# Two-layer cross attention: the load of x issued after those of Wv and Wo, a split product in the first layer's queries, and key bias sums over all 800 query columns

## The chip, the cores and the metric

The kernel runs on one core of one Trainium2 chip. The metric is the device time of one execution in microseconds (us). Everything is float32.

## The reference

Two cross-attention layers run one after the other. There are 8 batches of 100 queries of width 1024 (x), and a context of 1444 rows of width 512 for each batch.

```
layer 0:  Q = x Wq + bq;  K = ctx Wk + bk;  V = ctx Wv + bv
          x = x + softmax_over_context(Q K^T / 32) V Wo + bo
layer 1:  q = x Wq + bq;  k = ctx Wk + bk;  v = ctx Wv + bv
          w = softmax_over_queries(q k^T / 32)
          out = layernorm(w v + x) * gamma + beta
```

## The kernel before

**What is multiplied.** Keys and values are never formed. Each layer first multiplies weights with weights: Wq Wk^T (1024 x 512, named `qk0` and `qk1`), and in layer 0 also Wv Wo (512 x 1024, `vo0`). `queries` then multiplies the transposed x (`xT`, 1024 x 800 in eight blocks of 128 rows) with the first product. The result `g0T` or `g1T` (512 x 800, kept as two halves of 400 columns) meets the raw context in `scores` (line 823). The softmaxed scores meet the raw context in `weighted_rows` (line 794), and `project0` or `project1` brings that back to width 1024.

**Split products.** The large products are done in seven half-size products in place of eight, with sums of blocks made on VectorE before and after. `inner_product` splits one of these seven once more in the same way: it makes eight block sums (named S1, T1 and so on in the code), runs seven products of a quarter of the size through `half_product`, and adds each to its place. It gives control back after each of the seven, so that a caller can weave other matmuls between them. In `queries` of layer 0 the product `A22 T1` (name `g0_w`) goes through `inner_product`, woven with eight single matmuls of `X += S3 T3`. The last one, `Y += S4 B22` (lines 702 and 703), is a plain product: 8 matmuls of 128x128 on 400 columns, and two VectorE additions into `g0T`.

**Loads.** A `unit` is one of 10 SBUF buffers 1536 columns wide. `weight_products` loads eight pairs of row blocks into eight units: for `vo0` the pair is Wv (256 KB) and Wo (512 KB), lines 354 and 355, on the queue of SyncE (SP). It yields once after writing down the loads. `qk0` holds eight units when `vo0` asks for its eight, so two of `vo0`'s pairs have a buffer at once and six wait for `qk0` to give one back. `xT` is a buffer of its own, loaded in two halves of 1600 KB at line 714, between the loads of `qk0` and those of `vo0`.

**Bias sums.** `transferred_sum` adds up a weight matrix scaled by a bias: eight ScalarE activations (line 524) into eight tiles, and seven accumulating DMAs from GpSimd's queue (line 528), each 512 KB, in a tree. This is done for `qk0` (`L0_xattn_bk`) and for `vo0` (`L0_xattn_bv`). `block_sums` transposes such a sum and reduces it on VectorE; for `vo0` that is written after the fifth step of the queries (line 743). `key_bias_sums` forms, for each query, the sum over 1024 features of `xT` times one scalar for each partition: per half of 400 columns one multiply (line 577) and seven multiply-adds (line 579), each of which reads what the one before wrote. Both layers call it once per half; its tile `kb` has three buffers. `key_biases` transposes the two halves and reduces them.

**What sets the order.** TensorE's instructions keep the order in which they are written (`manual_schedule(engines={PE})`). The order on the other engines and on their DMA queues is laid down by a planner when the program is built. `tc.keep_in_program_order`, and `vector.in_order = True` for the operations that go through `vector`, pin an instruction behind the one written before it on its engine. PSUM has six banks in the pool `psum` (`bank`) and two in `psum2` (`bank2`); a name that asks for a bank waits until one has been drained.

**Layer 1.** Its queries end with the plain product, too. Its `key_bias_sums` are written after five steps of the queries and are not pinned, so VectorE does them wherever the planner put them.

Of the kernel before, what the change touches and what calls it, by code (L numbers as in the profile page):

```python
# [31 lines left out]
P = 128  # L32
# [23 lines left out]
def two_layer_cross_attention(ctx: ExitStack, tc: tile.TileContext, a: dict, out: bass.AP):  # L56
# [83 lines left out]
    def run(*parts):  # L140

        parts = list(parts)
        while parts:
            parts = [g for g in parts if next(g, parts) is not parts]
# [387 lines left out]
    def block_sums(name, t, sums, late=False):  # L532

        ins = nc.vector.transpose(t, t)
        if late:
            tc.keep_in_program_order(ins)  # L540
        nc.vector.tensor_reduce(sums, t.rearrange("p (c q i) -> p c q i", q=P // QD, i=QD), AX.X, ALU.add)

    def totals(name, sums, n):

        ps = bank(name)[:, : n * P // QD]
        nc.tensor.matmul(ps, same, sums.rearrange("p c q -> p (c q)"), start=True, stop=True)  # L546
        own = small.tile([P, 2 * EC, P // QD], F32, tag="own", name=f"{name}_own", bufs=1)[:, :n, :]
        mask = quarter.unsqueeze(1).to_broadcast([P, n, P // QD])
        nc.vector.tensor_tensor(own, ps.rearrange("p (c q) -> p c q", q=P // QD), mask, ALU.mult)
        got = const.tile([P, n], F32, tag=name, name=name)  # L550
        nc.vector.tensor_reduce(got, own, AX.X, ALU.add)
        return got
# [14 lines left out]
        nc.vector.tensor_scalar(got, ps[:, :2], SCALE, None, ALU.mult)  # L567
        return got[:, 0:1], got[:, 1:2]

    def key_bias_sums(name, t0, t1, wqbk):  # L570

        acc = work.tile([P, GT + P - T], F32, tag="kb", name=name, bufs=3)
        nc.gpsimd.memset(acc[:, GT:], 0.0)
        for k in range(EC):
            src = xT[:, k, t0:t1]
            if k == 0:
                nc.vector.tensor_scalar(acc[:, :GT], src, wqbk[:, k : k + 1], None, ALU.mult)
            else:
                nc.vector.scalar_tensor_tensor(
                    acc[:, :GT], src, wqbk[:, k : k + 1], acc[:, :GT], ALU.mult, ALU.add  # L580
                )
        return acc

    def key_biases(name, kb, bqbk):

        sums = quarter_sums(name)[:, :B, :]
        t = row(f"{name}_t").rearrange("p (b q j) -> p b q j", q=P // QD, j=QD)
        for g in range(B // G):

            src = bass.AP(kb[g].tensor, kb[g].offset, [list(kb[g].ap[0]), [T, G], [QD, P // QD], [1, QD]])  # L590
            vector.transpose(t[:, g * G : (g + 1) * G], src)
        vector.tensor_reduce(sums, t, AX.X, ALU.add)
        yield
        c = totals(name, sums, B)
        nc.vector.tensor_scalar(c, c, SCALE, bqbk, ALU.mult, ALU.add)
        yield c

    def queries(layer, w, u):

        H, nb, h = EC // 2, 2, GT // 2
        A11, A12, A21, A22 = ([w[:, k * H : (k + 1) * H, j * 256 : j * 256 + 256]] for j in range(2) for k in range(2))
        B11, B21, B12, B22 = ([xT[:, k * H : (k + 1) * H, g * GT : g * GT + GT]] for g in range(2) for k in range(2))
        S1, S2 = ([row(f"g{layer}_s{n}").rearrange("p (c l) -> p c l", c=H)] for n in (1, 2))
        T1, T2 = ([wide(f"g{layer}_t{n}")] for n in (1, 2))
        T3 = [work.tile([P, LC, GT], F32, tag="gT", name=f"g{layer}_t3", bufs=3)]
        dst = [work.tile([P, LC, GT], F32, tag="gT", name=f"g{layer}T_{g}", bufs=3) for g in range(2)]

        def put(r, g, banks):
            for j in range(2):
                c = 2 * r + j
                nc.scalar.activation(dst[g][:, c, :], banks[j][:, :GT], AF.Identity, bias=u[:, c : c + 1])  # L614

        def add(r, g, banks):
            for j in range(2):
                to = dst[g][:, 2 * r + j, :]
                vector.tensor_tensor(to, to, banks[j][:, :GT], ALU.add)

        def parts(R, G):
            def part(r, c, ps):
                return dst[G][:, 2 * R + r, c * h : c * h + h], ps[:, :h]

            def put(r, c, ps):
                c0 = 2 * R + r
                nc.scalar.activation(*part(r, c, ps), AF.Identity, bias=u[:, c0 : c0 + 1])

            def add(r, c, ps):
                to, got = part(r, c, ps)  # L630
                vector.tensor_tensor(to, to, got, ALU.add)

            return put, add

        def pair(n):
            return [bank(f"g{layer}_{n}{j}") for j in range(2)]

        def product(banks, lhs, rhs, fresh):
            half_product(banks, lhs, rhs, fresh, nb, GT)

        t = unit(f"g{layer}_t")

        def inner(n, lhs, rhs, put, add, right=None):
            return inner_product(f"g{layer}_{n}", lhs, rhs, nb, GT, t, put, add, right)

        def steps():
            X = pair("x")
            product(X, A11, B11, True)
            put(0, 0, X)
            yield  # L650
            S3, S4 = A21, A12
            if layer == 0:
                Z = pair("z")
                product(Z, A12, B21, True)
            vector.in_order = layer == 0
            combine(S1, A21, A22, ALU.add)
            vector.in_order = True
            combine(T1, B12, B11, ALU.subtract)
            combine(S2, S1, A11, ALU.subtract)
            if layer == 0:  # L660
                combine(T2, B22, T1, ALU.subtract)
                vector.in_order = False
                yield
                vector.in_order = True
                add(0, 0, Z)
            combine(S3, A11, A21, ALU.subtract)
            if layer == 0:
                combine(T3, B22, B12, ALU.subtract)
            Y = pair("y")
            product(Y, S1, T1, True)  # L670
            put(1, 1, Y)
            if layer:

                vector.in_order = False
                yield
                vector.in_order = True
                S4 = A11
                combine(S4, A12, S2, ALU.subtract)
                _, more = parts(0, 0)
                room = [[T3[0][:, n, :].rearrange("p (i t) -> p i t", i=2)] for n in range(4)]  # L680
                Z = inner("z", A12, B21, more, more, room)
                combine(T2, B22, T1, ALU.subtract)
                run(Z)
                combine(T3, B22, B12, ALU.subtract)
            else:
                combine(S4, A12, S2, ALU.subtract)
            combine(T1, B21, T2, ALU.subtract)
            vector.in_order = False
            yield
            product(X, S2, T2, False)  # L690
            put(0, 1, X)
            yield
            vector.in_order = True
            V = half_steps(X, S3, T3, False, nb, GT)
            for _ in inner("w", A22, T1, *parts(1, 0)):
                next(V)
            run(V)
            add(1, 0, X)
            add(1, 1, X)
            vector.in_order = False  # L700
            yield
            product(Y, S4, B22, False)
            add(0, 1, Y)
            yield

        return dst, steps()
# [2 lines left out]
    *_, (wqk0, (acc_c, acc_u)) = weight_products(  # L709
        "qk0", "L0_xattn_WqT", "L0_xattn_WkT", E, L, (("L0_xattn_bk", 0), ("L0_xattn_bq", 1))  # L710
    )
    xT = const.tile([P, EC, B * T], F32, tag="xT", name="xT")
    for g in range(B // G):
        nc.sync.dma_start(
            out=xT[:, :, g * GT : (g + 1) * GT],
            in_=a["xT"].rearrange("(c p) t -> p c t", p=P)[:, :, g * GT : (g + 1) * GT],
        )
    bqbk0, bqbk1 = bias_products()
    sums_u, sums_c = quarter_sums("u0")[:, :LC, :], quarter_sums("c0")

    def first_block_sums():
        block_sums("u0", acc_u, sums_u, late=True)
        block_sums("wqbk0", acc_c, sums_c[:, :EC, :], late=True)

    *_, (wvo, (acc_o,)) = weight_products(
        "vo0", "L0_xattn_WvT", "L0_xattn_Wo", L, E, (("L0_xattn_bv", 1),), first_block_sums
    )
    gT = [None, None]
    gT[0], steps = queries(0, wqk0, totals("u0", sums_u, LC))
    got = []  # L730

    def key_biases_begun():
# [6 lines left out]
    run(islice(steps, 2))  # L739
    next(qk1)  # L740
    next(qk1)
    run(islice(steps, 3))
    block_sums("bvo", acc_o, sums_c[:, EC:, :], late=True)
    run(steps)
    wqbk0 = totals("wqbk0", sums_c, 2 * EC)
    nc.vector.tensor_tensor(out_bias, out_bias, wqbk0[:, EC:], ALU.add)
    kb0 = [key_bias_sums(f"kb0_{g}", g * GT, (g + 1) * GT, wqbk0[:, :EC]) for g in range(B // G)]
    wqk1, (acc_c, acc_u) = next(qk1)
    c0 = next(got[0])
    for t in prob:  # L750
# [376 lines left out]

    gT[1], steps = queries(1, wqk1, u1)
    run(islice(steps, 5))
    kb1 = [key_bias_sums(f"kb1_{g}", g * GT, (g + 1) * GT, wqbk1) for g in range(B // G)]  # L1130
    *_, key_bias[1] = key_biases("c1", kb1, bqbk1)
    vectors = [unit(f"vectors_{j}") for j in range(2)]
    gamma, beta = (t[:, :E] for t in vectors)
# [57 lines left out]
```

## Time and profile before

| what | value |
|---|---|
| median of 3 runs | 635.54 us (635.3 to 635.9) |
| profiled execution | 638.23 us |
| its span, first to last instruction | 636.1 us |
| mean granted TensorE clock | 0.995 |
| TensorE busy | 623.6 us, 98% |
| VectorE busy | 469.7 us, 74% |
| ScalarE, GpSimd busy | 165.9 us, 98.9 us |
| DMA | 138.32 MB, mean 217 GB/s |

All durations come from the one profiled execution, whose time is 638.23 us: its span of 636.1 us and 2.13 us around it. A matmul in float32 shows as two records[...]. Matmul records overlap, so the time of a group of them is taken from one start to the next.

### The profile page before, as it was taken

Reading aid. Unit: us, or ns where it says so; the run is one execution under the profiler, and the core shown is the slowest. Engines: PE = TensorE matmul, PEld = TensorE weight load, DVE = VectorE, ACT = ScalarE, POOL = GpSimd, SP = SyncE. Lnnn points to the kernel's source line nnn. Section 1 sums busy time; section 2 is a strip of 40 time slices with the busy share of each in tenths; the row PEclk is TensorE's granted clock in tenths of the full one; section 3 lists DMA queues with packets and bytes.
Section 4 is the critical chain, followed back from the end, with each engine's and each line's share of the span. In section 5 each row is a group of like instructions: output and inputs, shape, how many; then the busy total and the mean of one; then the engine's idle time right before and its main releaser. Section 6 shows DMA issues by size and latency. Waiting matters only on the chain.

```text
span 636.1 us, 10422 instructions
## 1 busy us (share of the span) xinstructions
PE 623.6 (98%) x4100; PEld 529.5 (83%) x4100; DVE 469.7 (74%) x942; ACT 165.9 (26%) x377; POOL 98.9 (16%) x131
## 2 busy tenths in 40 slices
PE   9999899999999999999999999999999999999994
PEld 8886366678985999999998656756999999999992
DVE  2956779977884797676655699639777659898886
ACT  1524210105204244323230001113432240325301
POOL 3112110002300000000000001007211220544054
PEclk9999999999999999999999999999999999999998
DMA  8999987015789888998965206156788990599002
GB/s 275 333 281 355 219 199 245 1 47 96 136 281 385 285 302 300 331 307 310 311 222 186 95 1 231 48 181 202 280 304 304 312 316 28 197 327 332 31 20 85
DMA packets 51943, 138.32 MB, mean 217 GB/s; under 512 B 4339, under 2 KB 8691, under 8 KB 51895
## 3 DMA queue, kind: packets, MB, share of 16 engines
q1 hardware_dynamic: 46792, 120.85, 55.1%
q0 software_dynamic: 4704, 16.35, 11.3%
q8 instruction: 32, 0.52, 0.3%
q10 hardware_dynamic: 398, 0.47, 0.2%
q14 instruction: 17, 0.13, 0.1%
HBM read 123.36 MB, written 3.28 MB: 199 GB/s over the span
## 4 chain that ended last, share of the span: by engine, by line
PE 93%; DMA 4%; DVE 1%; POOL 1%; issue 1%; POOLq 0%; ACT 0%; DVEq 0%; SPq 0%
PE s L823 25%; PE A L794 24%; PE qk_x L163 6%; PE g_x L163 5%; PE o_x L163 5%; DMA vo<-in_L_xattn_Wo 4%; PE g_y L163 3%; PE o_y L163 3%; PE qk_y L163 2%; PE qk_z L163 2%; PE vo_x L163 2%; PE o_w L163 2%; PE o_z L163 2%; PE qk_w L163 1%; PE vo_y L163 1%; PE z L1022 1%
## 5 line engine op out<-in xcount | busy, mean ns | idle before, releaser
L794 PE MATMUL A<-w,c 120*128 120x100 f32 (+1 forms) x1536 | 247.9, 266 | 0.0
L794 PEld LDWEIGHTS A<-w,c 120*128 120x128 f32 (+1 forms) x1536 | 216.2, 191 | 0.8
L96 DVE STREAM_TRANSPOSE w<-prob 32x384 f32<-32x384 f32 (+1 forms) x256 | 143.7, 561 | 35.1 <-ACT prob L835 15.7
L823 PE MATMUL s<-cT,g1T 128*100 128x131 f32 (+2 forms) x592 | 123.1, 297 | 0.3 <-DVE g1T L96 0.3
L823 PE MATMUL s<-cT,g0T 128*100 128x131 f32 (+2 forms) x592 | 122.9, 297 | 0.0
L823 PEld LDWEIGHTS s<-cT,g1T 128*100 128x100 f32 x592 | 78.4, 168 | 9.2 <-DVE g1T L96 1.2
L823 PEld LDWEIGHTS s<-cT,g0T 128*100 128x100 f32 x592 | 78.3, 168 | 8.4 <-PE c L546 0.4
L835 ACT ACTIVATE prob<-s,c 100x393 f32<-100x393 f32 (+2 forms) x64 | 35.0, 560 | 112.8 <-PE s L823 112.5
L945 ACT ACTIVATE w<-w,negmax 120x100 f32<-120x100 f32 (+1 forms) x96 | 34.8, 364 | 82.3 <-DVE negmax L96 82.3
L855 DVE TENSOR_REDUCE maxima<-prob 100x1 f32<-100x394 f32 (+3 forms) x32 | 16.5, 528 | 24.2 <-ACT prob L835 24.0
L1140 POOL DMA_DIRECT2D wv<-in_L_xattn_Wv x1 | 0.8, 772 | 203.2 <-PE o_x L163 203.2
L163 PE MATMUL qk_x<-qk 128*128 128x256 f32 x128 | 30.2, 384 | 0.0
L964 POOL TENSOR_TENSOR part<-w 120x500 f32<-120x500 f32 x8 | 10.9, 1366 | 113.0 <-DVE rstd L1039 28.6
L163 PEld LDWEIGHTS qk_x<-qk 128*128 128x128 f32 x128 | 23.8, 194 | 3.0 <-ACT qk L413 0.2
L528 POOL DMA_DIRECT2D qk_L_xattn_bk<-qk_L_xattn_bk x8 | 6.9, 863 | 102.5 <-ACT qk_L_xattn_bk L524 80.8
L614 ACT ACTIVATE g1T<-g_x,k 128x400 f32<-128x400 f32 x4 | 2.4, 594 | 69.1 <-PE g_x L163 68.9
L96 DVE TENSOR_TENSOR xT<-xT,o_x 128x400 f32<-128x400 f32 (+1 forms) x32 | 16.0, 541 | 4.1 <-PE o_x L163 3.9
L945 ACT ACTIVATION_READ_ACCUMULATOR w<-w,negmax 120x1 f32 (+1 forms) x96 | 17.9, 186 | 0.0
L1044 POOL TENSOR_TENSOR z<-z,vectors 100x1024 f32<-100x1024 f32 x7 | 16.5, 2358 | 8.2 <-ACT z L1043 8.2
L1043 ACT ACTIVATE z<-z,rstd 100x1024 f32<-100x1024 f32 x7 | 8.0, 1149 | 31.9 <-POOL rstd L1040 31.9
L1022 PE MATMUL z<-ident,xT 128*100 128x128 f32 x64 | 16.3, 273 | 0.0
L96 DVE TENSOR_TENSOR w<-w,rtotal 120x400 f32<-120x400 f32 (+1 forms) x24 | 15.6, 648 | 0.7
(319 smaller groups left out, 961.2 us busy)
## 6 DMA issues: line engine op xcount, KB each, us to landing
cT<-in_ctxT SPq DMA_DIRECT2D x64, 722.0 KB, 6.9
c<-in_ctx SPq DMA_DIRECT2D x48, 768.0 KB, 8.9
c<-in_ctx SPq DMA_DIRECT2D x16, 512.0 KB, 7.7
qk_L_xattn_bk<-qk_L_xattn_bk POOLq DMA_DIRECT2D x8, 512.0 KB, 8.3
vo<-in_L_xattn_Wo SPq DMA_DIRECT2D x8, 512.0 KB, 9.2
qk<-in_L_xattn_WqT SPq DMA_DIRECT2D x8, 512.0 KB
qk<-in_L_xattn_WqT SPq DMA_DIRECT2D x15, 256.0 KB, 6.0
c<-in_ctx SPq DMA_DIRECT2D x16, 224.0 KB, 5.3
```

The costliest lines, as they stand in the source:

```text
L96: ins = getattr(nc.vector, op)(*args, **kw)
L163: nc.tensor.matmul(banks[n // per][:, n % per * width : (n % per + 1) * width], lhs[i][:, n * P : (n + 1) * P], rhs[i], start=(fresh and i ...
L528: nc.gpsimd.dma_start(out=tiles[i], in_=tiles[i + n], accum_op=ALU.add)
L794: nc.tensor.matmul(ps[:, k * T : (k + 1) * T], c[m // CQ][:r, m % CQ, k * P : (k + 1) * P], w[:r, m, :], start=(m == 0 and k == 0), stop=( ...
L823: nc.tensor.matmul(banks[n // per][:T, cuts[n] - o : cuts[n + 1] - o], q[:, k, t0 : t0 + T], cT[k][:, cuts[n] : cuts[n + 1]], start=(k == ...
L835: nc.scalar.activation(p[:, part], ps[:T, : part.stop - part.start], AF.Identity, bias=key_bias[layer][:T, b : b + 1], scale=SCALE,)
L855: nc.vector.tensor_reduce(maxima[:, n : n + 1], p[:, part], AX.X, ALU.max)
L945: nc.scalar.activation(w[:r, m0 + m, :], w[:r, m0 + m, :], AF.Exp, bias=negmax[:r, m : m + 1], accum_out=total[:r, m : m + 1])
L964: add(part, w[:MR, 0:5, :], w[:MR, 5:10, :], ALU.add)
L1022: nc.tensor.transpose(ps[:T, e * P : (e + 1) * P], xT[:, 4 * j + e, b * T : (b + 1) * T], ident)
L1043: nc.scalar.activation(z, z, AF.Copy, scale=rstd)
L1044: nc.gpsimd.tensor_tensor(z, z, beta[:T], ALU.add)
```

## The change

Three things are done.

1. The loads of `vo0` are written first, by the first step of `weight_products`, and the two halves of `xT` after them. The rest of `vo0` follows as before.
2. In layer 0 the last product of the queries, `S4 B22`, goes through `inner_product` under the name `q`, with the tile `T2` as room for its right-hand block sums. For that, `add(0, 1, Y)` moves ahead of it, into the loop over the steps of `w`; the first product of `q` is woven in before the last matmul of `X += S3 T3`, and the additions of `X` come behind the fifth of the seven. `block_sums("bvo", ...)` moves from its place behind the fifth step into that loop, as `between`. Layer 1 keeps the plain product.
3. `key_bias_sums` runs over all 800 columns at once: one multiply and seven multiply-adds in place of two and fourteen, in one buffer in place of three; `key_biases` transposes once.

```diff
-    def key_bias_sums(name, t0, t1, wqbk):
-        acc = work.tile([P, GT + P - T], F32, tag="kb", name=name, bufs=3)
+    def key_bias_sums(name, wqbk):
+        acc = work.tile([P, B * T + P - T], F32, tag="kb", name=name, bufs=1)
         for k in range(EC):
-            src = xT[:, k, t0:t1]
...
-                    acc[:, :GT], src, wqbk[:, k : k + 1], acc[:, :GT], ALU.mult, ALU.add
+                    acc[:, : B * T], xT[:, k, :], wqbk[:, k : k + 1], acc[:, : B * T], ALU.mult, ALU.add
...
-            for _ in inner("w", A22, T1, *parts(1, 0)):
+            for n, _ in enumerate(inner("w", A22, T1, *parts(1, 0))):
                 next(V)
...
+                if layer == 0 and n == 1:
+                    between()
+                elif layer == 0 and n == 3:
+                    add(0, 1, Y)
+                    _, more = parts(0, 1)
+                    Q = inner("q", S4, B22, more, more, four(T2[0]), 768)
+            if layer == 0:
+                next(Q)
+                run(V)
+                yield
+                run(islice(Q, 4))
+                add(1, 0, X)
+                add(1, 1, X)
+                run(Q)
+                vector.in_order = False
+            else:
...
+vo0 = weight_products(
+    "vo0", "L0_xattn_WvT", "L0_xattn_Wo", L, E, (("L0_xattn_bv", 1),), first_block_sums
+)
+next(vo0)
 xT = const.tile([P, EC, B * T], F32, tag="xT", name="xT")
 for g in range(B // G):
     nc.sync.dma_start(
...
+*_, (wvo, (acc_o,)) = vo0
...
-run(islice(steps, 3))
-block_sums("bvo", acc_o, sums_c[:, EC:, :], late=True)
 run(steps)
...
-kb0 = [key_bias_sums(f"kb0_{g}", g * GT, (g + 1) * GT, wqbk0[:, :EC]) for g in range(B // G)]
+kb0 = key_bias_sums("kb0", wqbk0[:, :EC])
...
-kb1 = [key_bias_sums(f"kb1_{g}", g * GT, (g + 1) * GT, wqbk1) for g in range(B // G)]
+kb1 = key_bias_sums("kb1", wqbk1)
```

More of the change, by code (lines that the diff above doesn't have):

```diff
@@ L568, in bias_products @@
         return got[:, 0:1], got[:, 1:2]
-    def key_bias_sums(name, t0, t1, wqbk):
-        acc = work.tile([P, GT + P - T], F32, tag="kb", name=name, bufs=3)
-        nc.gpsimd.memset(acc[:, GT:], 0.0)
+    def key_bias_sums(name, wqbk):
+        acc = work.tile([P, B * T + P - T], F32, tag="kb", name=name, bufs=1)
+        nc.gpsimd.memset(acc[:, B * T :], 0.0)
         for k in range(EC):
-            src = xT[:, k, t0:t1]
             if k == 0:
-                nc.vector.tensor_scalar(acc[:, :GT], src, wqbk[:, k : k + 1], None, ALU.mult)
+                nc.vector.tensor_scalar(acc[:, : B * T], xT[:, k, :], wqbk[:, k : k + 1], None, ALU.mult)
             else:
                 nc.vector.scalar_tensor_tensor(
-                    acc[:, :GT], src, wqbk[:, k : k + 1], acc[:, :GT], ALU.mult, ALU.add
+                    acc[:, : B * T], xT[:, k, :], wqbk[:, k : k + 1], acc[:, : B * T], ALU.mult, ALU.add
                 )
@@ L587, in key_biases @@
         t = row(f"{name}_t").rearrange("p (b q j) -> p b q j", q=P // QD, j=QD)
-        for g in range(B // G):
-            src = bass.AP(kb[g].tensor, kb[g].offset, [list(kb[g].ap[0]), [T, G], [QD, P // QD], [1, QD]])
-            vector.transpose(t[:, g * G : (g + 1) * G], src)
+        src = bass.AP(kb.tensor, kb.offset, [list(kb.ap[0]), [T, B], [QD, P // QD], [1, QD]])
+        vector.transpose(t, src)
         vector.tensor_reduce(sums, t, AX.X, ALU.add)
@@ L596, in key_biases, with queries @@
         yield c
-    def queries(layer, w, u):
+    def queries(layer, w, u, between=None):
         H, nb, h = EC // 2, 2, GT // 2
@@ L641, in queries, with inner, four @@
         t = unit(f"g{layer}_t")
-        def inner(n, lhs, rhs, put, add, right=None):
-            return inner_product(f"g{layer}_{n}", lhs, rhs, nb, GT, t, put, add, right)
+        def inner(n, lhs, rhs, put, add, right=None, at=0):
+            return inner_product(f"g{layer}_{n}", lhs, rhs, nb, GT, t[:, at:], put, add, right)
+        def four(t):
+            return [[t[:, n, :].rearrange("p (i t) -> p i t", i=2)] for n in range(4)]
         def steps():
@@ L679, in steps @@
                 _, more = parts(0, 0)
-                room = [[T3[0][:, n, :].rearrange("p (i t) -> p i t", i=2)] for n in range(4)]
-                Z = inner("z", A12, B21, more, more, room)
+                Z = inner("z", A12, B21, more, more, four(T3[0]))
                 combine(T2, B22, T1, ALU.subtract)
@@ L694, in steps @@
             V = half_steps(X, S3, T3, False, nb, GT)
-            for _ in inner("w", A22, T1, *parts(1, 0)):
+            for n, _ in enumerate(inner("w", A22, T1, *parts(1, 0))):
                 next(V)
[L697 to L703, printed above, removed]
+                if layer == 0 and n == 1:
[14 more added lines that the diff above has]
+            else:
+                run(V)
+                add(1, 0, X)
+                add(1, 1, X)
+                vector.in_order = False
+                yield
+                product(Y, S4, B22, False)
+                add(0, 1, Y)
             yield
@@ L711, in two_layer_cross_attention, with first_block_sums @@
     )
+    bqbk0, bqbk1 = bias_products()
+    sums_u, sums_c = quarter_sums("u0")[:, :LC, :], quarter_sums("c0")
+    def first_block_sums():
+        block_sums("u0", acc_u, sums_u, late=True)
+        block_sums("wqbk0", acc_c, sums_c[:, :EC, :], late=True)
+    vo0 = weight_products(
+        "vo0", "L0_xattn_WvT", "L0_xattn_Wo", L, E, (("L0_xattn_bv", 1),), first_block_sums
+    )
+    next(vo0)
     xT = const.tile([P, EC, B * T], F32, tag="xT", name="xT")
@@ L717, in two_layer_cross_attention @@
         )
[L718 to L726, printed above, removed]
-    )
-    gT = [None, None]
-    gT[0], steps = queries(0, wqk0, totals("u0", sums_u, LC))
+    *_, (wvo, (acc_o,)) = vo0
+    gT = [None, None]
+    gT[0], steps = queries(
+        0, wqk0, totals("u0", sums_u, LC), lambda: block_sums("bvo", acc_o, sums_c[:, EC:, :], late=True)
+    )
     got = []
```

## The prediction

> **What bounds the kernel now.** I read the page's busy times first, then who TensorE waited for, then the chain that ended last.
>
> ```profile
> PE 623.6 (98%) x4100; PEld 529.5 (83%) x4100; DVE 469.7 (74%) x942; ACT 165.9 (26%) x377; POOL 98.9 (16%) x131
> ...
> PE vo_z L163 <- DMA vo<-in_L_xattn_Wo: 2.8, 1, 2.8
> PE warm L108 <- DVE ones L105: 1.1, 1, 1.1
> PE s L823 <- DVE g1T L96: 0.3, 1, 0.3
> ```
>
> The second part (engine, what it waited for: total, times, longest) is complete: TensorE stands still 4.2 us in all. So only two things gain time: less work on TensorE, or the 2.8 us of waiting for Wo in `vo0`. Everything else is cover. The chain, in order of time (start, us, what), shows both places:
>
> ```profile
> 43.72 9.32 DMA vo<-in_L_xattn_Wo
> 53.08 14.77 DMA vo<-in_L_xattn_Wo
> 67.98 1.96 PE vo_z L163 x4
> ...
> 132.45 0.68 PE g_w_x L163 x4
> 133.12 1.34 PE g_x L163 x4
> 134.47 5.37 PE g_y L163 x16
> ```
>
> The last Wo block, issued at 53.08, lands at 67.85, and `vo_z` wanted it at 65.2. `g_y` at 134.47 is the product that the change splits. Third, SP's queue in order of time: x goes out at 17.81, two pairs of Wv and Wo behind it, and then SP stands for 13 us until `qk0` gives buffers back.
>
> ```profile
> 17.81 1.08 SPq L714 DMA_DIRECT2D xT<-in_xT  x2
> 19.03 5.19 SPq L354 DMA_DIRECT2D vo<-in_L_xattn_WvT  x1
> 24.27 1.10 SPq L355 DMA_DIRECT2D vo<-in_L_xattn_Wo  x1
> 25.42 0.48 SPq L354 DMA_DIRECT2D vo<-in_L_xattn_WvT  x1
> 25.95 2.57 SPq L355 DMA_DIRECT2D vo<-in_L_xattn_Wo  x1
> 41.62 0.33 SPq L354 DMA_DIRECT2D vo<-in_L_xattn_WvT  x1
> ```
>
> In stretches of 2 us the DMA share is 0.9 to 1.1 from 2 to 72 us, without a gap. What sets the landing of the last Wo is thus the bytes ahead of it, not its issue.
>
> [...] the seventh Wo landed at 61.42, 1.9 us after the sixth, when SP's queue was nearly alone; the eighth took 6.4 us more, with two accumulating DMAs of GpSimd's queue (issued from 57.35) under way. [...] three linked multiply-adds of 400 columns in layer 1 take (1.94-0.63)/2 = 0.655 us each, two chains in turn in layer 0 (7.73-0.63)/13 = 0.546 us.
>
> **Part 1, the order of the loads.** No DMA is added; two (3.28 MB) move. Written order would put them behind all eight pairs. But the planner does not keep written order where an instruction is ready early. In GpSimd's order of time:
>
> ```profile
> 5.46 0.20 POOL L138 MEMSET prob<- 128x4 f32 x3
> 5.56 0.26 POOL L573 MEMSET kb<- 128x28 f32 x3
> 23.88 0.92 POOL L528 DMA_DIRECT2D qk_L_xattn_bk<-qk_L_xattn_bk  x1 [18.07 <-ACT qk_L_xattn_bk L524]
> ```
>
> Line 573 is written far behind the accumulating DMAs of line 528 (one of the three belongs to layer 1), needs no input, and ran at 5.56 us because its buffer was free; the fourth, for which none was, ran at 178.4. The load of x needs no input either, its buffer is free from the start, and it isn't pinned. When SP has issued the second pair, the third has no buffer until about 41 us. So I take it that x goes out there, at about 21 us, behind two pairs of eight. Nothing on SP waits behind it in that gap.
>
> Then the same bytes lie ahead of the last Wo: 6.29 MB of `qk0`, x, and the pairs. DMA stays busy without a gap, the buffers come back when TensorE gives them (41.62 to 52.7), and the wait stays. The first two pairs land some 10 us earlier than 45.7 and 48.9, and TensorE wants them at 53 and later. Value: 0. The bounds are -2.76 (x behind all eight) and +2.25 (a third accumulating DMA of `vo0` gets in ahead, priced below).
>
> **Part 2, the split product.** TensorE: 8 matmuls of 400 columns, 16 records in 5.37 us, go. Seven products of 2 matmuls on 200 columns come, 4 records each, 0.68 us each by the rows of `g_w` (0.672 between starts): 4.7 us. Gain 0.65 us on the path. In layer 1 the same seven stand alone in `g_z` at 0.68, so weight loads don't slow them.
>
> VectorE gets eight block sums (four of 256 columns at 0.34, four of 400 at 0.48, from start to start in `g_w`): 3.3 us; and eight additions of 200 columns at 0.28: 2.2 us. The two additions of Y stay and only move. The cover:
>
> ```profile
> 131.88 0.36 DVE L96 TENSOR_TENSOR g0T<-g0T,g_w_y 128x200 f32<-128x200 f32 x1 [3.01 <-PE g_w_y L163]
> ```
>
> 3.0 us idle here and 0.9 before the next. I lay the pinned order on the clock of before. The block sums of `w` end at 127.6. The transpose and reduction of `bvo` (1.17 and 1.14) end at 129.9, the additions of Y (moved) at 131.0, the first four sums of `q` at 132.6. The additions of `w` follow as TensorE delivers, to 133.7. The first product of `q` ends at 134.5; its addition and two sums end at 135.6, wanted by the fourth product at 136.5. The next pair ends at 137.0; TensorE wants its first half, done at 136.6, at 137.2. Slack 0.5 to 0.9 us: no wait. The four additions of X run from 138.2 to 140.1 and give back the banks of X. `qk1`'s first product would start at 139.4 and needs its second bank at 140.2; the first of X is free at 139.6. Slack 0.6 us. If the planner puts a filler of `qk1` (0.34 to 0.61 us) in the wrong place, TensorE waits some tenths: 0 to +1.0, taken +0.1.
>
> **Part 3, the key bias sums.** VectorE only. In layer 0 they took 141.64 to 150.04, 8.4 us. One chain of 800 exposes the link at each step: [...] 8.0 us. So the gain is 0.4 us on VectorE, not half. They end at about 149.8, since part 2 ends 0.5 us later on VectorE. TensorE next wants VectorE's sums for `qk_y` at 153.2, chunk by chunk; up to 3 us of these remain: near, but covered.
>
> In layer 1 a step over 800 columns needs both halves of `xT`, and blocks 4 and 5 of the second half are finished at about 384 and 385.
>
> ```profile
> 386.22 1.94 DVE L579 SCALAR_TENSOR_TENSOR kb<-xT,k,kb 128x400 f32<-128x400 f32 x3
> 388.27 0.71 DVE L96 STREAM_TRANSPOSE c_t<-kb 128x512 f32<-128x512 f32 x1
> 389.01 1.22 DVE L96 TENSOR_REDUCE c_sums<-c_t 128x32 f32<-128x1024 f32 x1
> 390.15 1.22 DVE L96 TENSOR_TENSOR qk<-qk,g_s 128x1024 f32<-128x1024 f32 x1
> ...
> 395.70 0.36 DVE L96 TENSOR_TENSOR g1T<-g1T,g_z_x 128x200 f32<-128x200 f32 x1 [0.96 <-PE g_z_x L163]
> ```
>
> Before, five steps of 400 came after 384.02; now four of 800 must (about 4.2 us with their links, against 3.1), and one transpose of 1.17 for two (1.33). So the sum at 390.15, which the split `g_z` needs, starts up to 0.9 us later. The 0.96 us idle at 395.70 takes that: 0, with bounds -0.1 and +1.0. Without that cover it is one for one, for TensorE already waits 0.3 us in `g_z` on this chain.
>
> **Sum.** 0 - 0.65 + 0.1 = -0.55 us. The profiled execution would go from 638.23 (span 636.1) to 637.7; the median, 2.7 us lower than the profiled time, from 635.54 to 635.0.
>
> **The rivals.** A: x really goes out behind all eight pairs. Then the DMA engines have 3.28 MB less ahead of Wo. By 28 us they had moved 8.7 MB; without x they run out at about 35.5 us, 6 us before the next buffer. From 41.62 on, 4.72 MB of pairs and up to 2.1 MB of accumulations at the 325 GB/s of 42 to 68 us take 21 us: the last Wo lands at about 63 at the latest, and `vo_z` wants it at 65.2. The wait goes, x lands before 80 and is wanted at 102.6. 635.0 - 2.8 = 632.2. For it: the written order. Against it: the memsets.
>
> B, slower: the first two pairs land early, ScalarE scales them early, and a third accumulating DMA of `vo0` is issued before the last Wo lands. Its price is (6.4-1.9)/2 = 2.25 us, estimated from the two that were under way. 635.0 + 2.25 = 637.25; it decides from 1.9 us of extra wait on. For it: GpSimd's queue was held by the tree of `qk0` until 56.81, after the first tiles of `vo0` were ready. Against it: the third step needs the first two landed, or tile 5, scaled only at 60.6.
>
> C: a bank or a late block sum in part 2, or the chain of 800 in layer 1, costs TensorE more than the split gains: 1.0 to 1.7 us of new waits, 636.2 (up to 636.9). For it: slacks of 0.5 to 1 us at four places. Against it: each of these holds on paper.
>
> **How the numbers follow.** Forecast 0.58, A 0.19, B 0.14, C 0.09. A measurement of this kernel tells 0.2%, 1.27 us, from no change. The forecast's own range is 634.2 to 636.2; 0.52 of it is no change and 0.06 faster (a wait for Wo that shrinks). A is faster. B is slower. C is 0.04 no change and 0.05 slower. Faster 0.25, same 0.56, slower 0.19. The range of 8 in 10, 632.2 to 637.2, cuts A and B in half and leaves out a few in a hundred beyond.
>
> **What would show it.** SP's order of time: x between the second and third pair (part 1), or behind the eighth at about 54 us (A). TensorE's wait for Wo: 2.8 as before, none (A), about 5 (B). `g_q` in seven pieces of 0.68 us and no new wait of `g_q` or `qk_x` on VectorE or on a bank. The multiply-adds of 800 columns at about 1.07 us from start to start. `g_z` in layer 1 without more than 0.3 us of waits. The prediction is wrong if x is where it is written, or if VectorE's order around 128 to 141 us is another than the one laid out.

## The result, and the profile after

| | median | runs | all runs |
|---|---|---|---|
| before | 636.01 us | 20 | 635.01 to 641.68 |
| changed | 641.42 us | 20 | 634.05 to 644.48 |

The ratio of changed to before is 1.0055, with a 95% interval of 1.0031 to 1.0079: slower, by half a per cent. It compares mean times, 640.79 with 637.27 us, and leaves out the two longest runs of the changed kernel, which count as slow; the medians differ by 5.4 us. The prediction was 635.0 us, with a range of 632.2 to 637.2. Both kernels scatter by several us, and the scatter belongs to the case: 6 of the 20 runs of before lie above 638 us, and 19 of the 20 of the changed kernel.

The profiled execution of the changed kernel took 640.21 us, its span is 638.4 us and its mean granted clock 0.992. First, whom TensorE waited for (engine, what it waited for: total us, times, longest):

```profile
PE vo_z L163 <- DMA vo<-in_L_xattn_Wo: 4.5, 1, 4.5
PE warm L108 <- DVE ones L105: 1.1, 1, 1.1
PE s L843 <- DVE g1T L96: 0.3, 1, 0.3
```

There is no new entry. The old one, the wait for the last Wo, grew from 2.8 to 4.5 us. The chain in order of time (start, us, what) passes the same two loads as before:

```profile
43.09 12.17 DMA vo<-in_L_xattn_Wo
55.27 13.65 DMA vo<-in_L_xattn_Wo
```

The fourth Wo, out at 43.09, takes 12.17 us where it took 9.32. The last one goes out when the fourth has landed, as before, so at 55.27 where it was 53.08. Behind it comes the surprise: the four records of the last pair of `vo_z` take 3.63 us, against 1.96 before. TensorE's own order of time has the wait in brackets, and the windows of 1 us (length, TensorE's busy time and records, granted clock, DMA share, GB/s) have the reason:

```profile
69.06 3.63 PE L163 MATMUL vo_z<-vo 128*128 128x512 f32 x4 [4.47 <-DMA vo<-in_L_xattn_Wo]
```

```profile
67.00:68.00 1.00, 0.00 (x0) 1.00 1.10 268
...
69.00:70.00 1.00, 0.94 (x1) 0.51 1.07 258
...
72.00:73.00 1.00, 1.00 (x3) 0.79 0.44 170
```

After standing for 4.47 us TensorE ran at half its clock (0.50 to 0.51) for 3.4 us. Before, after 2.76 us, the clock stayed at 1.00. In this execution the longer wait cost 1.67 us once more, after it was over.

SP's queue in order of time shows that x went where the prediction put it, between the second pair and the third:

```profile
19.83 0.33 SPq L355 DMA_DIRECT2D vo<-in_L_xattn_Wo  x1
20.85 2.47 SPq L743 DMA_DIRECT2D xT<-in_xT  x2
40.99 0.34 SPq L354 DMA_DIRECT2D vo<-in_L_xattn_WvT  x1
```

The split product is as laid out, in pieces of 0.67 us (0.84 us of record, overlapping), with some 0.15 us more around `g_q_w` (139.08, 139.82 and 140.57 are the starts from the piece ahead of it on). In layer 1 VectorE's order of time answers to the rows shown of before:

```profile
387.94 3.23 DVE L578 SCALAR_TENSOR_TENSOR kb<-xT,k,kb 128x800 f32<-128x800 f32 x3
391.27 1.25 DVE L96 STREAM_TRANSPOSE c_t<-kb 128x1024 f32<-128x1024 f32 x1
392.44 1.18 DVE L96 TENSOR_TENSOR qk<-qk,g_s 128x1024 f32<-128x1024 f32 x1
...
398.05 0.36 DVE L96 TENSOR_TENSOR g1T<-g1T,g_z_x 128x200 f32<-128x200 f32 x1
```

Three linked steps of 800 columns take 3.23 us, (3.23 - 1.04)/2 = 1.09 us from start to start, and the idle 0.96 us ahead of the addition of `g_z_x` is used up. With the span longer by 2.3 us, the sum at 392.44 stands where it stood (390.15).

The bill of the two profiled executions: wait +1.71, half clock +1.67, split product -0.50 (from the start of `vo_y` to that of `qk_x` 69.57 us, where it was 70.07; weighed below), and TensorE was done with the pair ahead of the last one 0.63 us earlier (65.22 to 64.59), the cause of which is open. That makes +2.25 of the +2.3 us in the span.

### The profile page after: what moved, and what is told of

The parts are those of the page before. It is cut to its first block, busy times and chain, and to the rows that moved or that the text cites. A ratio compares the mean times of both kernels' runs of the same rounds, so it can differ in the third digit from the quotient of the medians.

```text
span 638.4 us, 10446 instructions
## 1 busy us (share of the span) xinstructions
PE 624.2 (98%) x4112; PEld 530.7 (83%) x4112; DVE 472.5 (74%) x940; ACT 165.8 (26%) x377; POOL 98.8 (15%) x129
## 4 chain that ended last, share of the span: by engine, by line
PE 90%; DMA 4%; DVE 3%; issue 1%; POOL 1%; POOLq 0%; ACT 0%; DVEq 0%; SPq 0%
PE s L843 25%; PE A L814 24%; PE qk_x L163 6%; PE o_x L163 5%; PE g_x L163 4%; DMA vo<-in_L_xattn_Wo 4%; PE o_y L163 3%; PE qk_z L163 2%; PE qk_y L163 2%; PE vo_x L163 2%; PE g_y L163 2%; PE o_z L163 2%; PE o_w L163 2%; PE qk_w L163 1%; PE vo_y L163 1%; PE z L1042 1%
```

## Where the loss comes from: part 1 or the rest

**e1_order_only** is the kernel before with part 1 alone. **e2_rest_only** is the changed kernel with x loaded where it was, that is, parts 2 and 3 alone.

```diff
 e1_order_only, against the kernel before
-    xT = const.tile(...)
-    for g in range(B // G): nc.sync.dma_start(...)
...
+    next(vo0)
+    xT = const.tile(...)
+    for g in range(B // G): nc.sync.dma_start(...)
+    *_, (wvo, (acc_o,)) = vo0
```

```diff
 e2_rest_only, against the changed kernel
+    xT = const.tile(...)
+    for g in range(B // G): nc.sync.dma_start(...)
     bqbk0, bqbk1 = bias_products()
...
     next(vo0)
-    xT = const.tile(...)
-    for g in range(B // G): nc.sync.dma_start(...)
```

> The kernel before with the changed order of loads alone (x behind the second pair of Wv and Wo, as the planner puts it); queries and key bias sums as before. Theory W (the new place of x makes the last Wo land later; TensorE stands longer than 4 us, and then runs at half clock for some 3 us): 5 us slower than before, about 641 us, wait of vo_z for Wo 4 us or more, and records of vo_z at double length. Theory V (the loss is in the split product or in VectorE's sums, and the longer wait is chance, since the kernel before also has executions of 640 us): within 1 us of before, with the same mixture of times.

> The changed kernel with x loaded where it was, ahead of Wv and Wo: split product and wide key bias sums alone. Theory W: 0.65 us faster than before, about 635.3 us, wait for Wo 2.8 us as before. Theory V: slower than before, up to 5 us, with new waits of TensorE in g_q, qk_x or qk_y.

e1_order_only: 642.77 us (640.8 to 644.38), ratio 1.0084 [1.0064, 1.0104], wait for Wo 4.8 us, and after it a granted clock of 0.58 and 0.56 in the windows from 70 to 72 and from 72 to 74 us. e2_rest_only: 636.7 us (634.06 to 641.49), ratio 1.0003 [0.9977, 1.0029], and no wait for Wo at all in its profiled execution (634.96 us), where theory W had 2.8; 8 of its 20 runs lie above 638 us. So the loss is part 1's. Parts 2 and 3 can't be weighed against a scatter of 7 us.

## Is it the place of x in the queue, and what does the half clock cost?

**e3_x_behind_all** is the changed kernel with the two loads of x pinned, so that they stand behind all eight pairs (rival A of the prediction). **e4_kept_busy** has five matmuls that nobody reads ahead of the last pair of `vo_z`; they only fill the wait.

```diff
 e3_x_behind_all, against the changed kernel
-        nc.sync.dma_start(out=xT[...], in_=...)
+        tc.keep_in_program_order(nc.sync.dma_start(out=xT[...], in_=...))
```

```diff
 e4_kept_busy, against the changed kernel
-            product(Z, A12, B21, True)
+            zs = half_steps(Z, A12, B21, True, nb, rh)
+            run(islice(zs, 3 * nb))
+            fill = bank("fill")
+            for _ in range(5):
+                nc.tensor.matmul(fill, units[4][:, :P], units[4][:, l_width : l_width + 512], ...)
+            run(zs)
```

> The changed kernel with the two loads of x pinned in written order behind all eight pairs. Theory W: no wait for Wo in vo_z (last Wo lands at about 63 us), no stretch at half clock: 632.2 us and little spread from execution to execution. Rival: the last Wo still lands after 65 us, since the two accumulating DMAs issued at 57 us set it and not the bytes of x: 635 us or more, with a wait of 1 us or more. Theory V: 3 us or more above 632.2 although no wait for Wo is left.

> The changed kernel with five extra matmuls of 128x128 on 512 columns (4.3 us, into a bank that nothing reads) ahead of vo_z's last pair, so that TensorE isn't idle while it waits for the last Wo. It tells the half clock from the wait. If standing still is what lowers the clock: no records at half clock, the remaining wait under 1 us, and 1.7 to 3 us faster than the changed kernel, about 638.5 to 639.5 us. If the clock has nothing to do with standing still: the stretch at half clock stays, and the time is that of the changed kernel (641.4) or above.

e3_x_behind_all: 636.81 us (636.05 to 639.08), ratio 0.9984 [0.9963, 1.0004]. That is 4.6 us less than the changed kernel, but 4.6 us more than the 632.2 that rival A was given. TensorE still waits, now at the sixth pair:

```profile
63.89 5.76 PE L163 MATMUL vo_z<-vo 128*128 128x512 f32 x12 [1.99 <-DMA vo<-in_L_xattn_Wo]
```

The accumulating DMAs of `vo0` started at 47.21 and 53.92 in this kernel, since its first pairs landed early, and from 54 to 62 us, in windows of 2 us, the DMA engines moved only 246 to 290 GB/s. The 325 GB/s that rival A took from the kernel before didn't hold, and the last Wo landed at 67.7 us, not by 63.

e4_kept_busy: 640.16 us (638.15 to 645.83), ratio 1.0049 [1.0024, 1.0074]. The median is 1.3 us under the changed kernel's 641.42, but the two were not measured side by side, and by the ratios (1.0049 against 1.0055) a gain in time is not shown. TensorE's order of time, the filling matmuls and the last pair behind them:

```profile
66.21 4.46 PE L468 MATMUL fill<-vo 128*128 128x512 f32 x10
71.50 1.96 PE L163 MATMUL vo_z<-vo 128*128 128x512 f32 x4 [0.83 <-DMA vo<-in_L_xattn_Wo]
```

The last Wo came later still (71.4), yet the last pair took 1.96 us at a clock of 1.00. So in this case it is standing still that lowers the clock, and as an estimate (1.67 us of the 5.4 between the medians) that is the smaller part of the loss. What the filling saves is less in some runs: five of the 20 took 642.8 to 645.8 us, at a mean clock of 0.991 to 0.994, where the other 15 have 0.995 to 0.998. What makes Wo late was still only argued: the accumulating DMAs beside it.

## The accumulating DMAs of vo0 held back

In these four kernels the accumulations of `vo0` go out from the last tiles to the first, pinned. The first of them then waits until the last Wo has landed and been scaled, and none of them is under way while Wv and Wo are loaded. Work and bytes are the same. The edit is put on the kernel before (e5), on e2_rest_only (e6), on the changed kernel (e7) and on e3_x_behind_all (e8).

```diff
 e5 to e8, in transferred_sum
-            for i in range(0, EC, 2 * n):
-                nc.gpsimd.dma_start(out=tiles[i], in_=tiles[i + n], accum_op=ALU.add)
+            order = range(0, EC, 2 * n)
+            for i in reversed(order) if name.startswith("vo0") else order:
+                ins = nc.gpsimd.dma_start(out=tiles[i], in_=tiles[i + n], accum_op=ALU.add)
+                if name.startswith("vo0"):
+                    tc.keep_in_program_order(ins)
```

> The kernel before, with one thing added: the accumulating DMAs of vo0 go out from the last tiles to the first and are pinned in that order, so that none of them is under way while SP still loads Wv and Wo. Same work, same bytes. Theory W (what delays the last Wo is that SP's queue shares the DMA engines with the first accumulations of vo0): the last Wo, issued at about 53, lands some 2 us after the seventh, by 64 us; no wait of vo_z above 0.3 us, no half clock, span about 633.3 and 635 or less, and nearly the same time in every run (within 1.5 us). Rival R (the last Wo is late because of where its issue stands in SP's queue, or because of the bytes ahead of it): the wait for Wo stays at 1 us or more in the profile, and the time at 636 to 637 with its spread.

> Parts 2 and 3 alone (x at its old place), with the accumulations of vo0 held back as in e5_hold_before. With the wait for Wo out of the way this weighs parts 2 and 3. My prediction had -0.65 us on TensorE and +0.1 us of new waits, and the traces showed 0.35 us less outside the span: e5_hold_before minus 0.5 to 1.0 us, about 634. A rival: they cost as much as they gain, and this is within 0.2 us of e5_hold_before.

> The changed kernel with the accumulations of vo0 held back. Theory W: x behind the second pair costs only by way of the race of the last Wo with the accumulations of vo0; without the race the last Wo, issued at about 55, lands by 65 us, the wait is under 0.5 us, and the time is that of e6_hold_rest within 0.4 us, about 634: a ratio of 0.995 to the kernel before and 0.988 to the changed one. Rival L: the later issue of the last Wo (55.3 against 53.1) is enough to make it late: it lands at 66 us or later, vo_z waits 1 us or more, and the time stays 1 to 4 us above e6_hold_rest.

> x pinned behind all eight pairs (as in e3_x_behind_all), with the accumulations of vo0 held back. In e3_x_behind_all the sixth Wo came at 63.86 beside accumulations issued at 47.2 and 53.9. Theory W: without them every Wo lands as soon as its buffer is free, the wait of 2.0 us goes, and the time is that of e7_hold_after within 0.4 us. Rival: the wait in e3_x_behind_all came from the buffers (each given back by qk0 when TensorE is done), not from the rate: then 1 us or more of it stays.

| kernel, accumulations held | us | all runs | without the hold | ratio to before |
|---|---|---|---|---|
| e5: before | 635.44 | 634.57 to 636.43 | 636.29 | 0.9965 [0.9947, 0.9983] |
| e6: parts 2 and 3 | 635.28 | 634.35 to 636.42 | 636.70 (e2) | 0.9971 [0.9955, 0.9986] |
| e7: changed | 635.97 | 633.80 to 636.59 | 641.42 | 0.9980 [0.9961, 0.9999] |
| e8: x behind all pairs | 634.44 | 633.72 to 635.30 | 636.81 (e3) | 0.9957 [0.9940, 0.9974] |

Except for before, the times without the hold were not measured beside these; the medians of before beside them lie between 636.0 and 636.8 us. By its wait of 1.26 us e5 meets the mark of rival R, by its time and its narrow spread that of theory W. The scatter is gone in all four (none of 88 runs above 638), and the changed kernel loses 5.45 us (0.0075 in the ratio) by an edit that leaves its load order alone. So the loss of part 1 is the race of the last Wo with the accumulations of `vo0`: what counts is how far these get ahead of it.

How it works is seen in the distance from the sixth landing of a Wo to the last, read from ScalarE's order of time (each activation of line 524 starts when its Wo lands), and in what the queues moved in between (queue, kind: packets, MB, share of 16 engines; q0 is GpSimd's queue, q1 is SP's). The changed kernel:

```profile
59.27 1.15 ACT L524 ACTIVATE prob<-vo,L_xattn_bv 128x1024 f32<-128x1024 f32 x1 [0.89 <-DMA vo<-in_L_xattn_Wo]
69.00 1.15 ACT L524 ACTIVATE prob<-vo,L_xattn_bv 128x1024 f32<-128x1024 f32 x1 [5.84 <-DMA vo<-in_L_xattn_Wo]
q0 software_dynamic: 353, 1.31, 67.6%
q1 hardware_dynamic: 478, 1.41, 39.0%
```

The kernel before, the queues alone (from 59.48 to 67.93):

```profile
q0 software_dynamic: 281, 1.05, 62.4%
q1 hardware_dynamic: 458, 1.39, 43.5%
```

e7_hold_after, whose sixth Wo landed at 59.45:

```profile
65.69 1.15 ACT L524 ACTIVATE prob<-vo,L_xattn_bv 128x1024 f32<-128x1024 f32 x1 [2.01 <-DMA vo<-in_L_xattn_Wo]
q0 software_dynamic: 144, 0.52, 42.1%
```

In e8_hold_x_behind_all q0 moved nothing between the landings:

```profile
58.58 1.15 ACT L524 ACTIVATE prob<-vo,L_xattn_bv 128x1024 f32<-128x1024 f32 x1 [1.13 <-DMA vo<-in_L_xattn_Wo]
62.48 1.15 ACT L524 ACTIVATE prob<-vo,L_xattn_bv 128x1024 f32<-128x1024 f32 x1 [0.79 <-DMA vo<-in_L_xattn_Wo]
```

SP's queue moved nearly the same in each, the two last pairs. The distance follows q0: 3.9 us with nothing of GpSimd's queue (the tree of `qk0` was issued by 47.66 already in e8), 6.2 to 6.3 us in e5, e6 and e7 with 0.52 MB, one accumulation (the last of `qk0`), 8.5 us in the kernel before with 1.05 MB, 9.7 us in the changed one with 1.31 MB. As an estimate from these, each accumulation that gets ahead of the last Wo costs about 2.3 us. My expectation that the last Wo of e5 lands some 2 us after the seventh (it took 4.3) overlooked the last accumulation of `qk0`. It explains the wait of 1.26 us that stayed in the profile of e5 and the 0.63 us in that of e7; no run takes this one accumulation away alone. e6 and e8 have no wait.

The later issue of the last Wo isn't the cause by itself (rival L): issued at 55.45 us in e7 and at 53.62 in e6, it landed 6.2 us after the sixth in both. e7 is 0.7 us slower than e6 (means: 0.45 us): what the load order costs apart from the race is small. e8 lies 1.5 us under e7 (means: 1.3 us), where 0.4 was expected at most; the wait of 0.63 us is part of that, and the rest stays open. e5 and e6 lie only 0.16 us apart, the rival's mark of e6, which left parts 2 and 3 to be weighed where no Wo is waited for.

## Parts 2 and 3 weighed

The base is the kernel before with x pinned behind all pairs and the accumulations of `vo0` held (e9). Part 2 alone (e10), part 3 alone (e11) and both (e12, the same as e8) are put on it, all on one chip.

```diff
 the base, against the kernel before: the diffs of e1_order_only, e3_x_behind_all and e5
 e10: + queries() and the place of block_sums("bvo", ...) of the change
 e11: + key_bias_sums(), key_biases() and their calls of the change
 e12: + both
```

> The kernel before with x pinned behind all eight pairs and the accumulations of vo0 held back: e8_hold_x_behind_all without parts 2 and 3. It is the base on which they are weighed, since no Wo is waited for here. By the traces (from the start of vo_y to that of qk_x 70.07 us without and 69.56 us with the split product, from there to the end 0.1 us more with parts 2 and 3) parts 2 and 3 are worth 0.4 us: 634.85 if e8 gives 634.45 again. By the prediction's -0.55 it is 635.0. Rival: the two gain nothing, as e5_hold_before and e6_hold_rest suggest (0.16 apart): within 0.2 us of e8.

> e9_base with the split product alone: 0.5 us less than e9_base (0.65 predicted on TensorE); g_q in seven pieces of about 0.68 us with some 0.1 us of waits. If part 3 costs anything, this is the fastest of the four.

> e9_base with the key bias sums over 800 columns alone: by the prediction 0 (bounds -0.1 and +1.0), by the traces so far +0.1 us: equal to e9_base within 0.2 us, and no new wait of qk_y or g_z on VectorE.

> e8_hold_x_behind_all once more, beside the other three on the same chip: 634.4, equal to e10_base_part2 within 0.2 us, 0.4 us under e9_base, and two us or more under the kernel before on average.

| | us | all runs | runs | span, profiled |
|---|---|---|---|---|
| e9: base | 634.94 | 634.08 to 635.74 | 22 | 633.9 |
| e10: part 2 | 634.26 | 633.72 to 635.28 | 18 | 632.7 |
| e11: part 3 | 634.92 | 634.26 to 635.77 | 20 | 633.8 |
| e12: both | 634.51 | 633.68 to 635.33 | 17 | 632.8 |

The runs of one kernel spread by 0.5 us (standard deviation), so the difference of two medians is good to about 0.2 us (0.5 x 1.25 x the root of 2/20, one standard error). Part 2 gives -0.68 without part 3 and -0.41 with it, together about -0.55. Part 3 gives -0.02 and +0.25: nothing that this tells from zero. The traces agree. From the start of `vo_y` to the start of `qk_x` of `qk1`, TensorE's order of time has 137.63 - 67.56 = 70.07 us in e9 and 136.59 - 67.02 = 69.57 us in e10, a gain of 0.50; in e11 it is 70.06.

e10 has the lowest median of all: 634.26 us, a ratio to before of 0.9957 [0.9941, 0.9972], on whose chip before took 636.42. Its 0.25 us under e12 are no more than the noise. The changed kernel's 641.42, not measured beside it, lies 7 us above.

## Presence or lead?

**e13_half_held** is the changed kernel with one pair of tiles put first, so that the accumulations of `vo0` start when the sixth Wo has been scaled, and not when the fourth has. **e14_changed_again** is the changed kernel on the same chip.

```diff
 e13_half_held, against e7_hold_after
-            for i in reversed(order) if name.startswith("vo0") else order:
+            for i in sorted(order, key=lambda i: i != 4) if name.startswith("vo0") else order:
```

> The changed kernel with the accumulations of vo0 held back in part: the pair of tiles 4 and 5 goes first, so that the first of them is issued when the sixth Wo has landed and been scaled, at about 60.5 us in place of 56.6, and all of them from then on. Theory W with lead (what counts is how many of their bytes are moved ahead of the last Wo's): the last Wo lands 2 to 3 us earlier than in the changed kernel, at 65.5 to 67.5; the wait is 1 to 2.5 us, the clock is not halved, and the time lies between e7_hold_after and the changed kernel, 636 to 637.5, with few runs above 640. Rival (any accumulation of vo0 beside the last Wo costs the whole): wait of 4 us and more, half clock, 640 to 642.

> The changed kernel once more, beside e13_half_held on the same chip: 641 to 641.5, nearly every run above 638, as in the result.

e13_half_held: 636.23 us (635.54 to 637.44), ratio 0.998 [0.9957, 1.0003]. e14_changed_again: 642.34 us (641.45 to 642.87, 4 runs), ratio 1.0086 [1.0069, 1.0103], somewhat above the 641 to 641.5 expected. In e13 the accumulations of `vo0` went out from 61.77 on, after the sixth Wo had landed, with waits of 1.3 and 0.7 us. In e14 they went out from 57.24 on, 2.95 us ahead of it, with a wait of 5.1 us, and the last pair of `vo_z` took 3.75 us (1.96 in before). The sixth landing is the mark, since the accumulations delay the seventh as well (2.7 us behind the sixth in the changed kernel, 1.9 in before). Put beside the others, one profiled execution each:

| kernel | accumulations of `vo0` issued from | sixth Wo lands | ahead by | MB of q0 until the last Wo | last Wo after the sixth |
|---|---|---|---|---|---|
| e8 | behind all | 58.58 | none | 0 | 3.9 |
| e5, e6, e7 | behind all | 59.72, 58.96, 59.45 | none | 0.52 each | 6.3, 6.2, 6.2 |
| e13 | 61.77 | 60.33 | -1.44 | 0.68 | 6.6 |
| e2 | 57.74 | 59.33 | 1.59 | 0.66 | 6.2 |
| before | 57.35 | 59.48 | 2.13 | 1.05 | 8.5 |
| changed | 56.58 | 59.27 | 2.69 | 1.31 | 9.7 |
| e1 | 57.12 | 59.90 | 2.78 | 1.38 | 10.1 |
| e14 | 57.24 | 60.19 | 2.95 | 1.45 | 10.4 |

The lead decides, not the presence: in e2 both accumulations were issued nearly 8 us ahead of the last landing, and counted from the sixth it came no later than in e6, which holds them back. The kernel before lies only half a microsecond of lead away from e2 and pays 2 us for it, which fits its scatter: some tenths decide whether an execution pays. Why the lead is 0.6 to 0.8 us longer in the new order is not tested. The traces show that the sixth accumulation of `qk0` runs ahead (46.73 and not 48.06 us), so that it slows the fourth Wo and not the fifth, and that the last Wo, which goes out when the fourth has landed, is then issued 1.5 to 3 us later (55.27 to 56.19 in the changed kernel, e1 and e14, 53.08 and 53.79 in before and e2). How much of the loss is this later issue beside the accumulations, and how much the lead itself, no run separates.

## Why the prediction was wrong, step by step

**What bounds the kernel.** Right in its terms: TensorE and one wait. Wrong in one number that was in plain sight. The profiled time stood 2.7 us above the median, and the wait for Wo was 2.76 us. I carried the first as an offset. It was the wait itself: by their times most runs of before have little or nothing of it (e2, without it, took 634.96 us). The wait was not a constant of the kernel but a race that was won more often than lost.

**Part 1, place of x.** Right: behind the second pair, at 20.85 us for "about 21". **Part 1, value 0.** This is the step that failed: "the same bytes lie ahead of the last Wo ... and the wait stays". The bytes of SP's queue were the same (1.39 and 1.41 MB from the sixth landing to the last); those of GpSimd's queue that went ahead of the last Wo were not: 1.05 MB in the profile of before, itself an execution that lost the race, 0.66 in that of e2, which won it, and 1.31 to 1.45 in the three profiles with the new order (changed, e1, e14). The prediction had read from the trace that the two queues share the engines, and then took the share of the accumulations as fixed. The wait grew by 1.7 us between the two profiled executions, and, as an estimate, by about 4.5 us for the common run, which had little or none.

**The bound of +2.25.** Too small for a second reason: a wait was priced one for one, and the traces show more. TensorE's granted clock was halved after 4.47 us of standing (0.50 to 0.51, changed kernel), and after 4.82 us it was 0.58 and 0.56 in two windows of 2 us (e1); after 2.76 us (before) and 1.99 us (e3) it stayed at 1.00. It lasted 3.4 us in the changed kernel and, as an estimate from the two windows with 0.50 in them, 3.4 us in e1. In e14, after 5.11 us, the four records of the last pair of `vo_z` and the first three of `vo_y` took 6.2 us (70.61 to 76.85), twice as long as seven take at the 0.43 us from start to start that the records of `vo_y` have in before; why the slow stretch was longer there isn't shown. With the 1.67 us of the changed kernel's profile, the common run makes 4.5 + 1.67 - 0.5 = 5.7 us; the medians differ by 5.4, the means of all runs, which count the lost races of before too, by 3.8.

**Rival B**, given 0.14, came nearest, and it named the place, the sign and the signal (a wait of about 5 us). Its price of 2.25 us for one accumulation agrees with the 2.3 us between e8 and e5 to e7, in part by luck: the two it was worked out from were not the two of `vo0` but, in the order of the queue, the last of `qk0` and the first of `vo0`. Its mechanism was off by a detail: not a third accumulation of `vo0`, but more bytes of those already issued. **Rival A** had the place of x wrong for this kernel. Its price of 632.2 failed in e3, where the rate of 325 GB/s didn't hold, and would have failed without any wait: e8, in whose profile no Wo is waited for, took 634.44. The prediction took 2.8 us off a median that had little of this wait in it.

**Part 2.** Right: -0.65 + 0.1 predicted, -0.55 measured on the base, and 0.50 of it seen in the traces. VectorE's order was the one laid out, with three sums for `qk1` put in at 136.46; its four additions of X ran from 141.05 to 143.05 in the profile after, where the prediction's 138.2 to 140.1 come to lie within 0.2 us when moved by the 2.7 us that `vo_y` started later. **Part 3.** Right: nothing on the path. In layer 0 the eight steps did not run as one chain to about 149.8, though: the planner put sums for `qk1` between them, and they ended at 155.30 (152.6 by the clock of before), without a wait of TensorE for them. In layer 1 the step of 800 columns measured 1.09 us, for 1.07 expected. (The rows of before give 1.06 as an estimate: the linked step of 400 columns at 0.655 us, and 400 columns more at twice what an addition of 400 takes above one of 200, 0.48 - 0.28 us.) The cover of 0.96 us was used up, as said. The sum that I let slip by up to 0.9 us did not slip; the reduction went behind it instead (the sum starts at 392.44, the reduction at 393.88). Rival C did not come about.

## What to carry to other kernels

Where the profiled time and the median differ by as much as one wait of the profile, suspect that this wait is a race, lost in some runs and won in others, and ask what would make it be lost always, before pricing anything else. A load that the bottleneck waits for should have no transfers of another queue issued shortly ahead of it that nobody needs yet; here it took five lines that hold them back, and the scatter of 7 us went with the loss. A wait of TensorE can cost more than its length: here those of 4.47 us and more did, and one of 2.76 us did not; nothing in between was measured.

## What the runs showed of the hardware

Accumulating DMAs from SBUF to SBUF beside plain loads brought the moved bytes down from 416 to 418 GB/s (56 to 60 us, before) to 255 to 268 GB/s (62 to 68 us), in windows of 2 us with a DMA share of 1.04 to 1.07 in all. From 59.27 to 69.00 us of the changed kernel's profile, 1.31 MB of accumulations took 67.6% of the engines' time and 1.41 MB of plain loads 39.0% (records overlap): 1.9 times as long for each byte. Between the two last landings the plain loads were left with 0.79 MB (Wv and Wo of the last pair) in 7.0 us, 112 GB/s, about a quarter of what they get alone (1.93 us, 407 GB/s, in e8).

After TensorE had stood for 4.47 us, its granted clock was 0.50 to 0.51, for 3.4 us (changed kernel). After 4.82 us it was 0.58 and 0.56 in the two windows of 2 us that followed (e1), and after 5.11 us seven records took 6.2 us, 0.89 us each for 0.43 in before (e14). After 2.76 us (before) and 1.99 us (e3), and in e4 after 0.83 us, it was 1.00.

Around the span lie 2.13 us in before and 2.06 to 2.17 us in the runs of e1_order_only, and 1.72 to 1.89 us in those of the other kernels, except for three of e4_kept_busy with 2.1 us. No run explains it.
